# A graph-attention layer and a gated graph network: the ramp of a scheduled kernel, rearranged

## The chip, the cores and the metric

The kernel runs on one core of one Trainium2 chip. The metric is the device time of one execution in microseconds, as the median of several executions. An execution's time is a little longer than the span that its profile shows, from the first to the last instruction of the program.

## What is computed

The input is x, 32 sequences of 512 nodes with 128 features, in f32, and one adjacency matrix of 512 x 512 zeros and ones that all sequences share. Each of the two layers normalizes, clips at zero, runs a graph network and adds the result to its input:

```
h = max(layernorm(x), 0)
x = x + gat(h)          # layer 0
h = max(layernorm(x), 0)
x = x + ggnn(h)         # layer 1

gat(h):   hw = h @ W;  e_src = hw @ a_src;  e_dst = hw @ a_dst
          logits[i,j] = leaky_relu(e_src[i] + e_dst[j], 0.2)
          alpha = softmax over j, where adj[i,j] > 0
          return leaky_relu(alpha @ hw + b, 0.3)

ggnn(h):  five times:
          m = adj @ h                       # both halves of "av" are m
          z = sigmoid([m,m] @ w3.T + h @ u3.T + biases)
          r = sigmoid([m,m] @ w4.T + h @ u3.T + biases)
          v = tanh([m,m] @ w5.T + (r*h) @ u5.T + biases)
          h = (1-z)*h + z*v
```

## The kernel before

A sequence's 512 nodes are K = 4 groups of P = 128. The kernel doesn't write its instructions in the order of the loops. It makes a list of tasks first (`add`, line 320), each with an engine, the columns it works on, a key, the tasks it needs and the buffers it takes. A planner (`plan`, lines 79 to 129) then keeps a clock for each engine with the costs of `COST` (line 37), starts again and again the task that can begin first, and of those of one engine that can begin by then, the one with the lowest key. `at` holds a task back to a planned time. The tasks are issued in that order, and `pin` keeps the order of each engine as it was issued, so that each engine works through a queue fixed when the kernel is built, and waits where an operand isn't there yet. `BANKS` (line 48) counts the eight PSUM banks by use: m for aggregations, g for gates, v for candidates, o for all else.

**Before the first sequence.** SyncE (SP) issues the loads in the order x of sequence 0, the adjacency, x of 1 and 2, the weights, the biases (lines 413 to 418). ScalarE issues W (`gw`) and then the two score vectors a_src and a_dst (`avecs`, lines 394 to 396). TensorE has "idle" transposes (line 429): `FIRST_IDLE` of them may begin at a planned 700 ns, `IDLE` more at 8000, and their key of 1e12 lets any other work go first. The score vectors are spread over all partitions by a matmul with ones (`as_ps`, line 442), VectorE multiplies them with W and sums (`products`, line 452: wa = W a), and ScalarE writes wa beside W, which GpSimd (POOL) copied (lines 435 and 460 to 463). So `wrow` makes hw and the scores in one matmul. The adjacency is turned on TensorE in four blocks (`at_ps`, line 479), each copied from PSUM as f16 by ScalarE (`adjT`, line 487).

**Layer 0 of a sequence** (`layer0`, line 707) goes through these steps, each a task or a few:

- `relu_layernorm` (line 587): VectorE takes mean and variance of each group (599 to 606, ve is the variance plus epsilon), POOL raises ve to the power -0.5 (rs, line 614). With `first` (sequence 0), VectorE subtracts the mean (619) and then scales and clips all 512 columns (623). Otherwise VectorE makes nb = -mean * rs (630), and ScalarE scales, shifts and clips in four activations (638). It is used on x (names ending in a) and on x1, the result of layer 0 (names ending in b).
- `transposed` (line 648) turns h by four transposes on TensorE (655) and one ScalarE copy (658), for the first `DIRECT` = 4 sequences; later ones go through memory in blocks, by DMAs that POOL issues (`blockwise`, line 661).
- `product` (line 740): for each half of the groups, two matmuls make hp (749), and one ScalarE task takes the exponentials of the scores (755) and scales the two groups of hw by them (760).
- The exponentials of a node's scores are spread over the partitions (es): by transposes on TensorE for the first four sequences (`spread`, 774), through memory by POOL's DMAs (line and es) for the others.
- `weigh` (817): VectorE makes the weights pt of one group from es, hw and adjT; four of them. `average` (836): TensorE multiplies (av, 843), VectorE divides and adds the bias (rsum 870, o 872), then leaks (893) and adds x (896): x1.
- The second layer norm of x1, and its halves: hi is hN in f16 (ScalarE, 919), lo the remainder in f16 (VectorE, 917).

**Layer 1**, five steps of `recurrence` (line 923) for each sequence: TensorE aggregates hi and lo with adjT (m, 942), ScalarE copies (mT, 953), gates r and z (961, 962 and 982) and candidate (1000, 1001) follow with their tanh, and VectorE updates hT (974, 1012, 1018, 1021). hT is turned back on TensorE for the first and last sequences (1035), else through memory (1048 to 1059). Steps of several sequences are under way at once.

The instructions for an f32 matmul of the program appear twice in the profile, and those of its transposes once.

Of the kernel before, what the change touches and what calls it, by code (L numbers as in the profile page):

```python
# [15 lines left out]
P = 128  # L16
# [27 lines left out]
FIRST_IDLE, IDLE = 26, 30  # L44
# [234 lines left out]
def gat_then_gated_gnn_kernel(  # L279
# [40 lines left out]
    def add(*args, **kwargs):  # L320
        tasks.append(Task(*args, **kwargs))
        return tasks[-1]
# [71 lines left out]
    nc.scalar.dma_start(out=gw, in_=g_w)  # L394
# [19 lines left out]
    a_loaded = add("SP", [1], -9.8e9, lambda: load_rest("a"), lands=5800)  # L414
    xs[1] = load_x(1, -9.7e9, 6000)
    xs[2] = load_x(2, -9.6e9, 6200)
# [6 lines left out]
    f_idle = Buffer("o", "bank")  # L423
# [4 lines left out]
    for i in range(FIRST_IDLE + IDLE):  # L428
        add("PE", [480 if i < FIRST_IDLE else 256], 1e12, idle, (), (f_idle,),
            at=700 if i < FIRST_IDLE else 8000)  # L430
# [3 lines left out]
    def issue():  # L434
        pin(nc.gpsimd.tensor_copy(wrow[:, :D], gw))
        pin(nc.gpsimd.tensor_copy(wsrc[:, :D], gw))

    w_copied = add("POOL", [1], soon, issue, at=3600)
# [8 lines left out]
    t = add("PE", [1024], soon, issue, (), (f_as,), at=4100)  # L447
# [9 lines left out]
    wa_made = add("DVE", [150] * 2, -5.6 * STEP, issue, (t,), (f_as, f_products))  # L457
# [14 lines left out]
    def prepare_adjacency(c):  # L472

        f = Buffer("o", "bank")

        def turn():
            at_ps = new(f, f"at_ps{c}")
            for k in range(K):
                pin(nc.tensor.transpose(
                    at_ps[:, ts(k, P)],  # L480
                    a_sb[:, k, :].rearrange("p (q c) -> p c q", c=K)[:, c, :],
                    ident,
                ))

        t = add("PE", [512] * K, -4 * STEP + c, turn, (a_loaded,), (f,))
        adjacency.append(add(
            "ACT", [512], -4 * STEP + c, lambda: pin(nc.scalar.copy(adjT[:, c, :], f.tile)), (t,),
            (f,),
        ))
# [97 lines left out]
    def relu_layernorm(dst, src, which, keys, needs, buffers, first):  # L587
# [3 lines left out]
        def stats():  # L591
# [4 lines left out]
            st["nb"] = pools[3].tile([P, K], F32, tag="nb", name=f"nb_{which}")  # L596
# [6 lines left out]
        def aggr():  # L603
            for k in range(K):
# [4 lines left out]
            ))  # L609

        t = add("DVE", [128] * K, keys(0), stats, needs, buffers)
        t1 = add("DVE", [30] * K + [1], keys(1), aggr, (t,))
        t = add("POOL", [1, 1], keys(2),
                lambda: pin(nc.gpsimd.tensor_tensor(own["rs"], own["ve"], mhalf, ALU.pow)), (t1,))  # L614
        if first:
# [5 lines left out]
            def scale():  # L621
                by = own["rs"].rearrange("p (k o) -> p k o", o=1).to_broadcast([P, K, D])
                pin(nc.vector.scalar_tensor_tensor(dst(), dst(), 0.0, by, ALU.max, ALU.mult))

            t1 = add("DVE", [512], keys(2), centre, (t1,), buffers)
            return add("DVE", [512], keys(3), scale, (t, t1), buffers)


        def negated():
            pin(nc.vector.scalar_tensor_tensor(  # L630
                own["nb"], own["mv"][:, :, 0], -1.0, own["rs"], ALU.mult, ALU.mult
            ))

        t = add("DVE", [1], keys(3), negated, (t,))
# [8 lines left out]
        t = add("ACT", [280] * 2, keys(4), lambda: relu((0, 1)), (t,), buffers)  # L643
        return add("ACT", [280] * 2, keys(4), lambda: relu((2, 3)), (t,), buffers)
# [3 lines left out]
    def transposed(dst, src, which, keys, needs, buffers):  # L648

        f = Buffer("o", "bank")  # L650

        def turn():
            t_ps = new(f, f"t_{which}")
            for k in range(K):
                pin(nc.tensor.transpose(t_ps[:, ts(k, P)], src()[:, k, :], ident))

        t = add("PE", [256] * K, keys(0), turn, needs, (*buffers, f))
        return add("ACT", [512], keys(1), lambda: pin(nc.scalar.copy(dst(), f.tile)), (t,),
                   (*buffers, f))

    def blockwise(dst, src, which, keys, needs, buffers):
# [45 lines left out]
    def layer0(b):  # L707
# [21 lines left out]
        t = turn(hT, h, f"a{b}", keys, (t,), (f_h, f_hT))  # L729
# [10 lines left out]
        def product(half):  # L740
# [13 lines left out]
            def scale():  # L754
                pin(nc.scalar.activation(
                    hw()[:, 2 * half : 2 * half + 2, D:], hp2()[:, :, D:], AF.Exp
                ))
                for c in range(2):
# [3 lines left out]
            u = add("PE", [4 * (D + 3)] * 2, keys(half), multiply, (t, wrow_made), (f, f_hT))  # L762
            return add("ACT", [1, 160, 160], keys(1 + half), scale, (u,), (f, f_hw))

        made = [product(half) for half in range(K // 2)]
        base[0] = 12

        if direct:
            f_es = Buffer("o", "bank")

            def spread():
                es = new(f_es, f"es_{b}")
                for k in range(K):
                    pin(nc.tensor.transpose(
                        es[:, ts(k, P)], hw()[:, k, D + 1 : D + 2].to_broadcast([P, P]), ident
                    ))

            t = add("PE", [256] * K, keys(0), spread, made, (f_hw, f_es))
# [57 lines left out]
        def average(part):  # L836
# [40 lines left out]
            if direct:  # L877
                u = None
                for c in range(K):
                    u = add("PE", [4 * (D + 1)] * 2, keys(part), multiply_with(c),  # L880
                            (weighed[c], u), (f, f_hw, f_pts[c]))
            else:
                u = add("PE", [4 * (D + 1)] * 2 * K, keys(part), multiply, weighed,
# [22 lines left out]
        t = relu_layernorm(hN, lambda: x1, f"b{b}", keys, (t,), (f_hN,), b == 0)  # L906
        base[0] = 26
        halved = halves(b, hN, keys(0), (t,), (f_hN,))
        t = turn(lambda: hTs[b % SLOTS], hN, f"b{b}", keys, (t,), (f_hN,))
        return halved, t  # L910
# [326 lines left out]
```

## Time and profile before

| | |
|---|---|
| median of 3 runs | 1149.26 us (1147.39 to 1150.59) |
| the profiled execution | 1149.29 us, its span 1147.5 us |
| TensorE (PE) busy | 1137.7 us |
| VectorE (DVE) busy | 941.6 us |
| ScalarE (ACT) busy | 664.2 us |
| GpSimd (POOL) busy | 349.5 us |
| idle transposes on TensorE | 56, from 1.4 to 24.0 us of the span |

The page of a profile gives the busy time of each engine, the same in 40 slices, the DMA queues, the chain of work that ended last (followed back from the last instruction, at each step to what released it), and groups of like instructions with the idle time before them and what ended it. PE is TensorE's matmul side, PEld its loading of weights, which overlaps. Beside the page, the trace answers with timelines of any stretch, with the chain in order of time, and with busy times by stretches. A matmul's end is modelled, and matmuls overlap, so that the distance between two starts says more of TensorE's pace than a duration.

### The profile page before, as it was taken

The page shows a single profiled execution, that of the slowest core. Times are in us where ns is not written, and L with a number is a line of the kernel's source. Part 1 is how long each engine was busy: PE and PEld are TensorE (multiplying, and loading weights), DVE is VectorE, ACT ScalarE, POOL GpSimd, SP SyncE. Part 2 cuts the span into 40 slices and gives each one's busy share as a digit, 9 for nine tenths or more (in the row PEclk, how much of TensorE's full clock was granted, in tenths as well). Part 3 has the DMA queues.
Part 4 walks back from the last instruction along what each step waited for, and adds up shares of the span by engine and source line. Part 5 has one row for each costly group of instructions (what it writes and reads, how often), then busy time and mean ns, then how long its engine had stood idle before and what let it go on. Part 6 is the DMA issues. An engine that isn't in the chain of part 4 may idle for free.

```text
span 1147.5 us, 15090 instructions
## 1 busy us (share of the span) xinstructions
PE 1137.7 (99%) x4363; PEld 602.0 (52%) x4363; DVE 941.6 (82%) x2114; ACT 664.2 (58%) x1294; POOL 349.5 (30%) x501
## 2 busy tenths in 40 slices
PE   8999999999999999999999999999999999999998
PEld 8666555455455554545555454545555555444444
DVE  6879897878787987988988797889997988767664
ACT  5665556645655556565565756565556644555553
POOL 3354432242324325153243432135335331100000
PEclk9999999999999999999999999999999999999999
DMA  3123454444444544344444444444454443332311
GB/s 106 37 56 82 135 149 111 112 137 128 116 128 131 143 121 140 108 126 142 144 135 119 143 127 120 129 129 141 121 142 127 117 126 93 115 94 90 102 51 57
DMA packets 133915, 132.88 MB, mean 116 GB/s; under 512 B 22082, under 2 KB 97988, under 8 KB 133700
## 3 DMA queue, kind: packets, MB, share of 16 engines
q1 hardware_dynamic: 116208, 95.02, 26.4%
q0 software_dynamic: 17472, 36.79, 13.0%
q8 instruction: 36, 0.59, 0.2%
q14 instruction: 51, 0.42, 0.1%
q10 hardware_dynamic: 148, 0.07, 0.0%
HBM read 70.39 MB, written 61.40 MB: 115 GB/s over the span
## 4 chain that ended last, share of the span: by engine, by line
PE 93%; DVE 4%; ACT 1%; DMA 1%; issue 1%; SPq 0%; POOL 0%; ACTq 0%; DVEq 0%
PE m L942 23%; PE g L982 12%; PE g L961 11%; PE g L962 11%; PE v L1001 11%; PE v L1000 11%; PE av L843 9%; PE hp L749 2%; PE h L1035 0%; DVE hT L1021 0%; DVE pt L819 0%; DMA rows<-way 0%; DVE blocks L1048 0%; DMA avecs<-in_L_gnn_a_dst_dram 0%; DVE o L872 0%
## 5 line engine op out<-in xcount | busy, mean ns | idle before, releaser
L967 ACT ACTIVATE rs<-g,zrb 128x512 f32<-128x512 f32 x160 | 109.8, 687 | 144.8 <-PE g L962 139.1
L1006 ACT ACTIVATE hv<-v,vb 128x512 f32<-128x512 f32 x159 | 108.9, 685 | 110.7 <-PE v L1001 110.3
L982 PE MATMUL g<-mT,w3dT 128*128 128x512 f32 x320 | 164.0, 594 | 0.4 <-ACT rs L967 0.4
L961 PE MATMUL g<-hT,u3T 128*128 128x512 f32 x320 | 163.4, 592 | 0.0
L962 PE MATMUL g<-mT,w4sT 128*128 128x512 f32 x320 | 163.4, 592 | 0.0
L1000 PE MATMUL v<-mT,w5sT 128*128 128x512 f32 x318 | 162.4, 592 | 0.0
L1001 PE MATMUL v<-rh,u5hT 128*128 128x512 f32 x318 | 162.4, 592 | 0.0
L1012 DVE SCALAR_TENSOR_TENSOR d<-hv,hT 128x512 f32<-128x512 f32 x159 | 108.3, 681 | 64.6 <-ACT hv L1006 63.9
L942 PE MATMUL m<-adjT,lo 128*128 128x512 f16 x640 | 158.4, 379 | 0.4 <-DVE lo L917 0.3
L942 PE MATMUL m<-adjT,hi 128*128 128x512 f16 x640 | 157.7, 379 | 0.1
L989 ACT ACTIVATE zs<-g,zrb 128x512 f32<-128x512 f32 x160 | 109.7, 686 | 72.6 <-PE g L982 71.6
L953 ACT COPY mT<-m 128x512 f32<-128x512 f32 x160 | 93.6, 585 | 93.3 <-PE m L942 92.1
L974 DVE SCALAR_TENSOR_TENSOR rh<-rs,hT 128x512 f32<-128x512 f32 x160 | 108.4, 679 | 47.2 <-ACT rs L967 46.3
L843 PEld LDWEIGHTS av<-hw,pt 128*128 128x128 f32 x1024 | 123.2, 191 | 16.3 <-issue 10.0
L843 PE MATMUL av<-hw,pt 128*128 128x129 f32 x1024 | 124.4, 275 | 0.5 <-DVE pt L819 0.5
L1021 DVE SCALAR_TENSOR_TENSOR hT<-d,hT 128x512 f32<-128x512 f32 x159 | 109.7, 690 | 12.8 <-PE v L1001 0.5
L614 POOL TENSOR_TENSOR rs_b<-ve_b,mhalf 128x4 f32<-128x4 f32 x32 | 37.2, 1161 | 266.4 <-DVE ve_b L606 148.7
L1018 DVE SCALAR_TENSOR_TENSOR d<-zs,d 128x512 f32<-128x512 f32 x159 | 109.7, 690 | 4.8
L942 PEld LDWEIGHTS <-lo 128*128 128x128 f16 x640 | 62.4, 98 | 95.5 <-issue 38.2
L942 PEld LDWEIGHTS <-hi 128*128 128x128 f16 x640 | 62.6, 98 | 93.8 <-issue 37.1
L1048 DVE STREAM_TRANSPOSE blocks<-hT 128x512 f32<-128x512 f32 x146 | 102.9, 707 | 6.8 <-DMA way<-blocks 4.5
L962 PEld LDWEIGHTS g<-mT,w4sT 128*128 128x128 f32 x320 | 60.8, 190 | 76.5 <-issue 69.4
(133 smaller groups left out, 1447.1 us busy)
## 6 DMA issues: line engine op xcount, KB each, us to landing
way<-blocks SPq DMA_DIRECT2D x146, 256.0 KB, 2.1
rows<-way SPq DMA_DIRECT2D x584, 64.0 KB, 2.1
x<-in_x_dram SPq DMA_DIRECT2D x32, 256.0 KB, 2.9
out_dram<-res SPq DMA_DIRECT2D x31, 256.0 KB, 2.3
turn_a<-blocks_a POOLq DMA_DIRECT2D x112, 64.0 KB, 2.2
h0T<-turn_a POOLq DMA_DIRECT2D x28, 256.0 KB, 3.5
es<-line POOLq DMA_DIRECT2D x28, 256.0 KB, 4.0
turn_b<-blocks_b POOLq DMA_DIRECT2D x112, 64.0 KB, 2.2
```

The source lines that it names most:

```text
L843: pin(nc.tensor.matmul(avs()[:, i, :], lhsT=f_pts[c].tile[:, ts(2 * part + i, P)], rhs=hw()[:, c, : D + 1], start=start, stop=(c == K - 1) ...
L942: pin(nc.tensor.matmul(f_m.tile, lhsT=part[:, k, :], rhs=adjT[:, k, :], start=(first and k == 0), stop=(not first and k == K - 1),))
L961: pin(nc.tensor.matmul(g, lhsT=u3T, rhs=hT, start=True, stop=False))
L962: pin(nc.tensor.matmul(g, lhsT=w4sT, rhs=f_mT.tile, start=False, stop=True))
L967: pin(nc.scalar.activation(new(f_r, f"rs_{b}_{step}"), f_g.tile, AF.Tanh, bias=rb, scale=0.5))
L982: pin(nc.tensor.matmul(f_g.tile, lhsT=w3dT, rhs=f_mT.tile, start=False, stop=True, skip_group_check=True))
L989: pin(nc.scalar.activation(new(f_z, f"zs_{b}_{step}"), f_g.tile, AF.Tanh, bias=zb, scale=0.5))
L1000: pin(nc.tensor.matmul(v, lhsT=w5sT, rhs=f_mT.tile, start=True, stop=False))
L1001: pin(nc.tensor.matmul(v, lhsT=u5hT, rhs=f_rh.tile, start=False, stop=True))
L1006: pin(nc.scalar.activation(new(f_hv, f"hv_{b}_{step}"), f_v.tile, AF.Tanh, bias=vb))
L1018: pin(nc.vector.scalar_tensor_tensor(d, f_z.tile, 1.0, d, ALU.add, ALU.mult))
L1021: pin(nc.vector.scalar_tensor_tensor(hT, f_d.tile, 0.5, hT, ALU.mult, ALU.add))
```

## The change

Nothing of what is computed changes. The edits are these:

- The score vectors are ScalarE's first loads; W is loaded by SP, after x of sequence 0. ScalarE copies W into `wrow` and `wsrc` instead of POOL. Planned times of the loads and of the first tasks are set anew, and there are 32 and 36 idle transposes instead of 26 and 30, the second group from a planned 6500 ns; their bank is of kind v.
- Adjacency: the banks of kind g are used, blocks 1 and 3 are copied by VectorE, 0 and 2 by ScalarE, with new keys; blocks 2 and 3 are held back to a planned 9900.
- Layer norm: except for sequence 0's first, VectorE makes nm = -mean and POOL makes nb = nm * rs right after rs. Sequence 0's first scales in two halves. Sequence 0's second is no longer `first`: ScalarE's activations do it.
- Transposes of h are two tasks of two; for the first norm of sequence 0 the copy is in halves too.
- The exponentials of hw are a task of their own for each half, and the scalings follow as other tasks; for the first four sequences they need the exponentials of both halves. The averages need the scalings. es for those sequences takes a bank of kind g and is made in two tasks.

As the planner decides the order, the queues of all engines differ over their whole length; the last twenty instructions of TensorE stand in the same order. In the new queue of TensorE, the "idle" transposes stand at 19 places, the last after some 1840 rows of about 3970. The diff, cut to its core:

```diff
@@ -43,3 +43,3 @@
 }
-FIRST_IDLE, IDLE = 26, 30
+FIRST_IDLE, IDLE = 32, 36
 LANDING = 2600
@@ -393,3 +393,2 @@
-    nc.scalar.dma_start(out=gw, in_=g_w)
     for i, v in enumerate((g_asrc, g_adst)):
@@ -413,5 +412,6 @@
     xs = {0: load_x(0, -9.9e9, 3200)}
-    a_loaded = add("SP", [1], -9.8e9, lambda: load_rest("a"), lands=5800)
-    xs[1] = load_x(1, -9.7e9, 6000)
-    xs[2] = load_x(2, -9.6e9, 6200)
+    add("SP", [1], -9.85e9, lambda: pin(nc.sync.dma_start(out=gw, in_=g_w)))
+    a_loaded = add("SP", [1], -9.8e9, lambda: load_rest("a"), lands=5000)
+    xs[1] = load_x(1, -9.7e9, 5000)
+    xs[2] = load_x(2, -9.6e9, 5100)
     rest_loaded = add("SP", [1] * 6, -9.5e9, lambda: load_rest("rest"), (xs[2][1],), lands=3000)
@@ -422,3 +422,3 @@
-    f_idle = Buffer("o", "bank")
+    f_idle = Buffer("v", "bank")
@@ -429,3 +429,3 @@
         add("PE", [480 if i < FIRST_IDLE else 256], 1e12, idle, (), (f_idle,),
-            at=700 if i < FIRST_IDLE else 8000)
+            at=700 if i < FIRST_IDLE else 6500)
@@ -434,6 +434,6 @@
     def issue():
-        pin(nc.gpsimd.tensor_copy(wrow[:, :D], gw))
-        pin(nc.gpsimd.tensor_copy(wsrc[:, :D], gw))
+        pin(nc.scalar.copy(wrow[:, :D], gw))
+        pin(nc.scalar.copy(wsrc[:, :D], gw))
-    w_copied = add("POOL", [1], soon, issue, at=3600)
+    w_copied = add("ACT", [128, 128], soon, issue, at=4200)
     f_as, f_products = Buffer("o", "bank"), Buffer("d")
@@ -446,3 +446,3 @@
-    t = add("PE", [1024], soon, issue, (), (f_as,), at=4100)
+    t = add("PE", [1024], soon, issue, (), (f_as,), at=3900)
@@ -456,3 +456,3 @@
-    wa_made = add("DVE", [150] * 2, -5.6 * STEP, issue, (t,), (f_as, f_products))
+    wa_made = add("DVE", [150] * 2, -5.6 * STEP, issue, (t,), (f_as, f_products), at=4400)
@@ -473,3 +473,4 @@
-        f = Buffer("o", "bank")
+        f = Buffer("g", "bank")
+        key = (0.2 * c - 3.8) * STEP
@@ -484,7 +485,7 @@
-        t = add("PE", [512] * K, -4 * STEP + c, turn, (a_loaded,), (f,))
-        adjacency.append(add(
-            "ACT", [512], -4 * STEP + c, lambda: pin(nc.scalar.copy(adjT[:, c, :], f.tile)), (t,),
-            (f,),
-        ))
+        t = add("PE", [256] * K, key, turn, (a_loaded,), (f,), at=9900 if c > 1 else 0)
+        engine, copy = ("DVE", nc.vector.tensor_copy) if c % 2 else ("ACT", nc.scalar.copy)
+        adjacency.append(
+            add(engine, [512], key, lambda: pin(copy(adjT[:, c, :], f.tile)), (t,), (f,))
+        )
@@ -595,3 +596,5 @@
             st["rs"] = pools[3].tile([P, K], F32, tag="rs", name=f"rs_{which}")
-            st["nb"] = pools[3].tile([P, K], F32, tag="nb", name=f"nb_{which}")
+            if not first:
+                st["nm"] = pools[3].tile([P, K], F32, tag="nm", name=f"nm_{which}")
+                st["nb"] = pools[3].tile([P, K], F32, tag="nb", name=f"nb_{which}")
             own.update(st)
@@ -609,2 +612,4 @@
             ))
+            if not first:
+                pin(nc.vector.tensor_scalar(own["nm"], own["mv"][:, :, 0], -1.0, None, ALU.mult))
@@ -612,4 +617,8 @@
         t1 = add("DVE", [30] * K + [1], keys(1), aggr, (t,))
-        t = add("POOL", [1, 1], keys(2),
-                lambda: pin(nc.gpsimd.tensor_tensor(own["rs"], own["ve"], mhalf, ALU.pow)), (t1,))
+        def power():
+            pin(nc.gpsimd.tensor_tensor(own["rs"], own["ve"], mhalf, ALU.pow))
+            if not first:
+                pin(nc.gpsimd.tensor_tensor(own["nb"], own["nm"], own["rs"], ALU.mult))
+        t = add("POOL", [1, 1], keys(2), power, (t1,))
         if first:
@@ -620,16 +629,17 @@
-            def scale():
-                by = own["rs"].rearrange("p (k o) -> p k o", o=1).to_broadcast([P, K, D])
-                pin(nc.vector.scalar_tensor_tensor(dst(), dst(), 0.0, by, ALU.max, ALU.mult))
+            def scale(half):
+                def issue():
+                    two = slice(2 * half, 2 * half + 2)
+                    by = own["rs"][:, two].rearrange("p (k o) -> p k o", o=1)
+                    pin(nc.vector.scalar_tensor_tensor(
+                        dst()[:, two, :], dst()[:, two, :], 0.0, by.to_broadcast([P, 2, D]),
+                        ALU.max, ALU.mult,
+                    ))
+                return issue
             t1 = add("DVE", [512], keys(2), centre, (t1,), buffers)
-            return add("DVE", [512], keys(3), scale, (t, t1), buffers)
+            return [add("DVE", [256], keys(3), scale(i), (t, t1), buffers) for i in range(2)]
-        def negated():
-            pin(nc.vector.scalar_tensor_tensor(
-                own["nb"], own["mv"][:, :, 0], -1.0, own["rs"], ALU.mult, ALU.mult
-            ))
-        t = add("DVE", [1], keys(3), negated, (t,))
@@ -642,4 +652,6 @@
-        t = add("ACT", [280] * 2, keys(4), lambda: relu((0, 1)), (t,), buffers)
-        return add("ACT", [280] * 2, keys(4), lambda: relu((2, 3)), (t,), buffers)
+        return [
+            add("ACT", [280] * 2, keys(4), lambda: relu((0, 1)), (t,), buffers),
+            add("ACT", [280] * 2, keys(4), lambda: relu((2, 3)), (t,), buffers),
+        ]
@@ -647,3 +659,3 @@
-    def transposed(dst, src, which, keys, needs, buffers):
+    def transposed(dst, src, which, keys, needs, buffers, by_halves):
@@ -651,12 +663,23 @@
-        def turn():
-            t_ps = new(f, f"t_{which}")
-            for k in range(K):
-                pin(nc.tensor.transpose(t_ps[:, ts(k, P)], src()[:, k, :], ident))
+        def turn(half):
+            def issue():
+                t_ps = f.tile or new(f, f"t_{which}")
+                for k in range(2 * half, 2 * half + 2):
+                    pin(nc.tensor.transpose(t_ps[:, ts(k, P)], src()[:, k, :], ident))
+            return issue
-        t = add("PE", [256] * K, keys(0), turn, needs, (*buffers, f))
-        return add("ACT", [512], keys(1), lambda: pin(nc.scalar.copy(dst(), f.tile)), (t,),
-                   (*buffers, f))
+        def copy(of):
+            return lambda: pin(nc.scalar.copy(dst()[:, of], f.tile[:, of]))
-    def blockwise(dst, src, which, keys, needs, buffers):
+        t = [add("PE", [256] * 2, keys(0), turn(i), (needs[i],), (*buffers, f)) for i in range(2)]
+        if not by_halves:
+            t = add("ACT", [512], keys(1), copy(slice(0, N)), t, (*buffers, f))
+            return [t, t]
+        return [
+            add("ACT", [256], keys(1), copy(ts(i, N // 2)), (t[i],), (*buffers, f))
+            for i in range(2)
+        ]
+    def blockwise(dst, src, which, keys, needs, buffers, by_halves):
@@ -728,3 +751,3 @@
         turn = transposed if direct else blockwise
-        t = turn(hT, h, f"a{b}", keys, (t,), (f_h, f_hT))
+        t = turn(hT, h, f"a{b}", keys, t, (f_h, f_hT), b == 0)
@@ -753,3 +776,3 @@
-            def scale():
+            def exponentials():
                 pin(nc.scalar.activation(
@@ -757,2 +780,4 @@
                 ))
+            def scale():
                 for c in range(2):
@@ -761,6 +786,13 @@
-            u = add("PE", [4 * (D + 3)] * 2, keys(half), multiply, (t, wrow_made), (f, f_hT))
-            return add("ACT", [1, 160, 160], keys(1 + half), scale, (u,), (f, f_hw))
-        made = [product(half) for half in range(K // 2)]
+            needs = (t[half], wrow_made) if direct else (t, wrow_made)
+            u = add("PE", [4 * (D + 3)] * 2, keys(half), multiply, needs, (f, f_hT))
+            u = add("ACT", [1], keys(0.9 + 0.1 * half), exponentials, (u,), (f, f_hw))
+            return u, scale, f
+        made, scales, f_hps = zip(*(product(half) for half in range(K // 2)))
+        scaled = [
+            add("ACT", [160, 160], keys(2 + i), scales[i], made if direct else (made[i],),
+                (f_hps[i], f_hw))
+            for i in range(2)
+        ]
         base[0] = 12
@@ -768,12 +800,17 @@
         if direct:
-            f_es = Buffer("o", "bank")
+            f_es = Buffer("g", "bank")
-            def spread():
-                es = new(f_es, f"es_{b}")
-                for k in range(K):
-                    pin(nc.tensor.transpose(
-                        es[:, ts(k, P)], hw()[:, k, D + 1 : D + 2].to_broadcast([P, P]), ident
-                    ))
+            def spread(half):
+                def issue():
+                    es = f_es.tile or new(f_es, f"es_{b}")
+                    for k in range(2 * half, 2 * half + 2):
+                        pin(nc.tensor.transpose(
+                            es[:, ts(k, P)], hw()[:, k, D + 1 : D + 2].to_broadcast([P, P]), ident
+                        ))
+                return issue
-            t = add("PE", [256] * K, keys(0), spread, made, (f_hw, f_es))
+            t = None
+            for half in range(2):
+                t = add("PE", [256] * 2, keys(0), spread(half), (made[half], t), (f_hw, f_es))
         else:
@@ -880,5 +917,5 @@
                     u = add("PE", [4 * (D + 1)] * 2, keys(part), multiply_with(c),
-                            (weighed[c], u), (f, f_hw, f_pts[c]))
+                            (weighed[c], scaled[c // 2], u), (f, f_hw, f_pts[c]))
             else:
-                u = add("PE", [4 * (D + 1)] * 2 * K, keys(part), multiply, weighed,
+                u = add("PE", [4 * (D + 1)] * 2 * K, keys(part), multiply, (*weighed, *scaled),
                         (f, f_hw, *f_pts))
@@ -905,7 +942,7 @@
-        t = relu_layernorm(hN, lambda: x1, f"b{b}", keys, (t,), (f_hN,), b == 0)
+        t = relu_layernorm(hN, lambda: x1, f"b{b}", keys, (t,), (f_hN,), False)
         base[0] = 26
-        halved = halves(b, hN, keys(0), (t,), (f_hN,))
-        t = turn(lambda: hTs[b % SLOTS], hN, f"b{b}", keys, (t,), (f_hN,))
-        return halved, t
+        halved = halves(b, hN, keys(0), t, (f_hN,))
+        t = turn(lambda: hTs[b % SLOTS], hN, f"b{b}", keys, t, (f_hN,), False)
+        return halved, t[0] if direct else t
```

## The prediction

> **What bounds the kernel now.** I read the busy rows of the page first, then the chain of waits, then the same chain cut to the first 30 us, and last the table of busy time by stretches.
>
> ```profile
> PE 1137.7 (99%) x4363; PEld 602.0 (52%) x4363; DVE 941.6 (82%) x2114; ACT 664.2 (58%) x1294; POOL 349.5 (30%) x501
> ...
> PE 93%; DVE 4%; ACT 1%; DMA 1%; issue 1%; SPq 0%; POOL 0%; ACTq 0%; DVEq 0%
> ```
>
> TensorE carries 93% of the chain. A busy row hides holes, because matmuls overlap and fillers count as work. So I counted TensorE's lost time from its starts in the timeline: unbroken runs start a 128x128 f32 instruction every 0.109 us, 128x129 and 128x131 every 0.112, 128x512 f16 every 0.216, 128x512 f32 every 0.429; whatever a start lies beyond that, and every "idle" transpose whole, is lost. The span then splits into 1.4 us before the first start, 16.2 lost up to 45 us, 2.8 lost from there to the last start at 1142.7 (0.4 of it at 1139.8, the rest in a dozen holes of 0.1 to 0.6), 4.8 after that start, and 1122.3 of work that the change leaves alone. 1.4 + 16.2 + 2.8 + 4.8 + 1122.3 = 1147.5. Outside the ramp there are 2.8 us to win or lose; the ramp has 16.2, of which 13.2 by 24.7 us. Its chain:
>
> ```profile
> 1.76 4.41 DMA avecs<-in_L_gnn_a_dst_dram
> ...
> 6.30 1.19 PE as_ps L442 x2
> 7.49 2.11 PE idle L426 x9
> 9.60 0.85 PE at_ps L479 x4
> 10.46 0.85 PE t_a L655 x4
> 11.31 1.70 PE at_ps L479 x8
> 13.01 0.89 PE hp L749 x8
> 13.90 0.11 PE idle L426
> 14.01 0.48 PE at_ps L479 x4
> 14.49 0.44 PE idle L426 x4
> 14.93 0.44 PE es L774 x4
> 15.36 0.98 PE idle L426 x9
> 16.35 3.35 PE av L843 x28
> 19.70 0.02 issue
> 19.72 0.18 DVE rsum L870
> ```
>
> The columns are start, length and what. The last score vector lands at 6.17; everything up to hp stands in TensorE's queue behind it, and those transposes take 0.213 us each. hp's four (x8) take 0.112: TensorE doubled its speed at 12.80.
>
> ```profile
> 20.00:25.00 5.00, 4.91 (x44) 4.62 (x43) 4.83 (x19) 3.48 (x13) 0.81 (x1) 1.00 0.16 54
> 25.00:30.00 5.00, 4.60 (x31) 3.38 (x31) 4.88 (x12) 2.73 (x9) 0.57 (x1) 1.00 0.00 0
> ...
> 40.00:45.00 5.00, 4.16 (x29) 3.33 (x30) 4.86 (x17) 2.40 (x8) 2.26 (x3) 1.00 0.04 17
> ```
>
> After the stretch, the columns are its length and busy PE, PEld, DVE, ACT, POOL. From 20 us VectorE is full (4.8 of 5), so TensorE's last ramp holes are waits for VectorE: an earlier start counts only if VectorE too is ahead.
>
> [...] In the trace a_src, issued at 1.25, landed at 3.95, and a_dst, issued at 1.76, only at 6.17, among the packets of the adjacency (landed 6.36).
>
> **Part by part** (the profiled execution: 1149.29 us, its span 1147.5 and 1.8 around it; the median 1149.26 is the same).
>
> *Loads.* Without gw ahead, a_dst takes a_src's place on ACT's queue (1.25) and lands near 3.95. gw goes to SP behind x of sequence 0; its issue moves the adjacency and x of 1 and 2 by 0.42 (the issue of one load), to 6.8, 7.3 and 8.0. Sixteen fillers end at 1.36 + 16 x 0.213 = 4.8, so as_ps starts at 4.8 instead of 6.3, and the hole is gone. W's two copies on ScalarE (0.37 each, as its 128x128 scalings) lie between W's landing near 4.2 and wa at 6.6, when ScalarE has nothing else; without that cover they would delay the four wa copies by 0.7, still ahead of h0T. The other kinds of bank cost nothing: g's gates begin after 25 us.
>
> *Clock.* [...] I take 5.97. Then: as_ps to 5.97, nine fillers to 6.95, two adjacency blocks (8 x 0.12) to 7.9, t_a (4 x 0.109) to 8.35.
>
> *First sequence in halves.* VectorE and POOL are not last: products after as_ps at 6.1, rs_a at 6.58 as now, two halves of 0.36 done at 7.3. ScalarE's halves of h0T follow their two transposes (0.2 after the start of the second): about 0.37 each from its 0.59 for 512, done at 8.7 and 9.0. hp starts at 8.75 instead of 12.80: -4.05. At 9.39: hp at 10.4, -2.4.
>
> *Exponentials apart.* Now from hp to pt 2.7 us (12.81 to 15.49): the second exponential waits for two scalings (0.63). Without them es would be done 1.75 after hp's start, but VectorE must first finish norms a1 and a2 and an adjacency copy: 7.3 + 2 x (0.87 + 0.40 + 0.17) + 0.65 = 10.9, so 2.1: -0.55. The scalings (x4, about 1.2) end before the first averages' weights do.
>
> *Adjacency by two engines.* No row shows VectorE copying PSUM to f16. Between 0.59 (ScalarE's copy) and 0.75 (pt): 0.65. One of its two copies stands between pt 0 and pt 1: +0.65 there, with the three pts behind it. Now, averages end 1.5 after the last pt, as 32 x 0.112 is longer than four pts; then they follow it by 0.75. Together 0. rsum then starts at 15.3 instead of 19.72: -4.4.
>
> *Layer-norm bias by POOL.* A product 128x4: 0.18 by the row of zrb's product, between 0.1 and 0.3 (its 128x128 copy is 0.29); 63 of them, 11 us on an engine busy 349.5. Queued behind each are POOL's DMA issues (turn, line, es): 0.2 later, beside loads of 2 to 4 us. VectorE's nm costs what nb did (0.15), its waits for POOL (3.2 us, all told) go. For the second norm of sequence 0, VectorE loses centre and scale (2 x 0.69), ScalarE gains four activations (4 x 0.40): about 1 us later on that path, to which VectorE's 1.4 is the return. VectorE's sum: +1.3 copies, -1.4, 0.
>
> *Order and fillers.* There are 12 more fillers. They stand where TensorE's order has nothing ready; up to twelve times 0.109 = 1.3 would be lost if one stood ahead of ready work. Walking the new order on with the same durations: ve of norm b comes 4.4 after rsum as now, 19.7; pow and product (1.4 and 0.2, with 0.2 between) end at 21.5, four activations at 23.2, hi (0.6) at 23.8; TensorE has fillers and averages of sequence 1 meanwhile; m's high part runs 23.9 to 24.7, four averages follow, the low part ends near 26.0 instead of 29.7, with 16.1 us of real work issued by then where 29.7 has 14.2: 5.5 ahead. Part of it goes again where VectorE is full (about 19 us of its work from norm b of sequence 0 to the second low part, as now, and x of 3 and 4 with it) and to the late fillers; I keep 4.1. The last twenty instructions are in the same order, so the 4.8 stay. 1149.3 - 4.1 = 1145.2.
>
> **Rivals.** *Late clock:* [...] -2.4 at 9.39, -1.6 at 12.8: 1147 to 1148. [...] *Given back:* VectorE at 4.8 of 5 does the same work up to 45 us, so TensorE waits for it there as long as it gained; 1149. Against: VectorE itself starts its full stretch 4 us earlier. *Slower:* the scalings, now tasks behind the exponentials, come late for the averages of the 28 sequences whose rows go through memory. One such wait costs what the hole of 0.48 at 964.8 cost; in all 28, 13.4 - 4.1 makes 1158.5; it decides from 16 of them on (7.7, the gain and 3.4 more). Against: es takes 4.0 from issue to landing after the exponentials, scalings 0.63, ScalarE is 58% busy.
>
> **Numbers.** About 0.3%, 3.4 us, is what a measurement here tells from no change: faster means below 1145.8. Forecast 0.53 (1143.5 to 1146.5, a tenth of it above 1145.8); late clock 0.28; given back 0.10; slower 0.07; more than forecast (all 5.5 kept, fewer later holes; 1142.5) 0.02. Faster 0.48 + 0.02 = 0.50; slower 0.07; same 0.43. The range reaches over the first three cases, with the later holes 0.5 either way: 1142.5 to 1149.5.
>
> **What would show it.** as_ps near 4.8; the step from 0.213 to 0.109 at about 6; hp at 8.8, rsum at 15.3; 12 us lost up to 45 us instead of 16.2. Wrong if avecs still land after 5, if the step comes at 9 or later, if ScalarE's scalings release av, or if the holes after 45 us sum to more than 4.

## The result and the profile after

The changed kernel takes 1156.11 us (median of 5 runs, 1155.04 to 1158.41) where the kernel before takes 1149.26 (5 runs, 1147.39 to 1150.59): a ratio of 1.0069, with a 95% interval of 1.0058 to 1.0080. The prediction was 1145.2, with a range up to 1149.5.

The page of the changed kernel shows hardly anything: the same busy times, VectorE even 0.5 us less, POOL 27 us more.

```profile
PE 1139.0 (99%) x4375; PEld 601.3 (52%) x4375; DVE 941.1 (82%) x2116; ACT 661.9 (57%) x1299; POOL 376.4 (33%) x562
...
PE 86%; DVE 6%; DMA 3%; POOL 2%; ACT 1%; issue 1%; DVEq 0%; SPq 0%; POOLq 0%; ACTq 0%
```

The second line, the chain's shares, is the one that speaks: TensorE had 93% of the chain and has 86% now. VectorE, DMA and POOL took the rest, so TensorE must have waited for them. Counting TensorE's lost time from its starts, as the prediction did:

| us | before | after |
|---|---|---|
| ahead of the first start | 1.4 | 1.4 |
| lost up to 45 us | 16.2 | 11.8 |
| lost from 45 us to the last start | 2.8 | 12.8 |
| after the last start | 4.8 | 5.8 |
| work | 1122.3 | 1122.3 |
| span | 1147.5 | 1154.1 |

The ramp lost 4.4 us less, and the stretch behind it 10 more. First the ramp, in the chain of the changed kernel cut to its first 40 us (start, length, what):

```profile
1.37 3.68 PE idle L426 x16
5.04 1.15 PE as_ps L442 x2
6.19 2.11 PE idle L426 x9
8.31 1.42 PE at_ps L480 x8
9.73 0.45 PE t_a L668 x4
10.18 0.02 issue
10.20 0.38 ACT h0T L673
10.58 0.04 issue
10.62 1.16 PE hp L772 x8
```

The wait for the score vectors is gone, as_ps follows the fillers at once, and hp starts at 10.62 instead of 12.80. The busy times of the three stretches that the prediction showed of before (length, then PE, PEld, DVE, ACT, POOL) are now:

```profile
20.00:25.00 5.00, 5.00 (x47) 4.96 (x45) 4.93 (x18) 3.54 (x12) 1.22 (x2) 1.00 0.17 52
25.00:30.00 5.00, 5.00 (x35) 3.86 (x35) 4.68 (x26) 3.42 (x9) 2.80 (x4) 1.00 0.01 2
40.00:45.00 5.00, 5.00 (x26) 3.02 (x24) 2.67 (x14) 2.08 (x6) 2.53 (x4) 1.00 0.07 13
```

TensorE is full in all three, and from 40 to 45 VectorE no longer is. Now the later stretch. From 60 to 1130 us, TensorE of the kernel before has two holes of over 0.25 us; the changed kernel has eight (1.0 us at 477.8, 3.1 at 536.2, 0.7 at 565, 0.7 at 586, 0.6 at 672, 1.4 at 844, 1.1 at 876, 0.6 at 896). The longest shows how it comes about. First ScalarE's timeline, then the chain, both of the changed kernel (nb_b is the bias of the second layer norm, rs_b its power):

```profile
533.65 0.63 ACT L785 ACTIVATE hw<-hp,hw 128x128 f32<-128x128 f32 x2
536.61 0.88 ACT L648 ACTIVATE hN<-x,nb_b,rs_b 128x128 f32<-128x128 f32 x2 [2.33 <-POOL nb_b L621]
537.39 0.67 ACT L1043 ACTIVATE hv<-v,vb 128x512 f32<-128x512 f32 x1
537.96 0.16 ACT L778 ACTIVATE hw<-hp 128x6 f32<-128x6 f32 x1
538.15 0.63 ACT L785 ACTIVATE hw<-hp,hw 128x128 f32<-128x128 f32 x2
538.67 0.62 ACT L956 CAST hi<-rows 128x512 f16<-128x512 f32 x1
```

```profile
534.55 1.41 POOL rs_b L619
535.96 0.07 issue
536.03 0.56 POOL nb_b L621
536.58 0.03 issue
536.61 0.88 ACT hN L648 x2
537.48 0.57 ACT hv L1043
...
538.67 0.63 ACT hi L956
539.29 0.05 issue
539.34 1.69 PE m L979 x7
```

ScalarE's queue had reached the activation of a layer norm whose power POOL had not begun. It stood for 2.33 us, and behind it in the queue stood the copy hi of another sequence, for which TensorE waited: the line of TensorE's waits is

```profile
PE m L979 <- ACT hi L956: 3.3, 2, 2.9
PE g L1019 <- ACT rs L1004: 1.8, 3, 0.9
PE g L998 <- DMA hT<-turn_b: 1.5, 2, 0.9
```

(total, times, longest). The holes at 478, 586 and 896 have the same kind of chain: power, product, two or four activations of the norm, a gate's tanh (rs, L1004), TensorE. Those at 565 and 876 end with hT, which a DMA brings from memory, the one at 672 with a copy hi, the one at 844 with VectorE. ScalarE's waits for the bias, first in the kernel before and then in the changed one, are

```profile
ACT hN L638 <- DVE nb_b L630: 7.7, 9, 1.8
ACT h L638 <- DVE nb_a L630: 5.4, 6, 2.1
...
ACT h L648 <- POOL nb_a L621: 11.7, 8, 4.0
ACT hN L648 <- POOL nb_b L621: 10.7, 12, 2.3
```

They sum to 13.1 us before and 22.4 after.

### The profile page after: what moved, and what is told of

Read it like the earlier page. It is cut to its first block, busy times and chain, and to the rows that moved or that the text cites. A ratio compares the mean times of both kernels' runs of the same rounds, so it can differ in the third digit from the quotient of the medians.

```text
span 1154.1 us, 15378 instructions
## 1 busy us (share of the span) xinstructions
PE 1139.0 (99%) x4375; PEld 601.3 (52%) x4375; DVE 941.1 (82%) x2116; ACT 661.9 (57%) x1299; POOL 376.4 (33%) x562
## 4 chain that ended last, share of the span: by engine, by line
PE 86%; DVE 6%; DMA 3%; POOL 2%; ACT 1%; issue 1%; DVEq 0%; SPq 0%; POOLq 0%; ACTq 0%
PE m L979 21%; PE g L1019 11%; PE g L998 10%; PE v L1038 10%; PE g L999 10%; PE v L1037 10%; PE av L880 9%; PE hp L772 2%; PE idle L426 1%; DMA rows<-way 1%; DVE pt L856 1%; DVE blocks L1085 1%; POOL rs_b L619 1%; DVE hT L1058 1%; DVE d L1055 1%
## 5 line engine op out<-in xcount | busy, mean ns | idle before, releaser
L1004 ACT ACTIVATE rs<-g,zrb 128x512 f32<-128x512 f32 x160 | 109.7, 685 | 148.3 <-PE g L999 148.0
L979 PE MATMUL m<-adjT,hi 128*128 128x512 f16 x640 | 160.4, 379 | 3.3 <-ACT hi L956 3.3
L1058 DVE SCALAR_TENSOR_TENSOR hT<-d,hT 128x512 f32<-128x512 f32 x159 | 109.9, 691 | 12.5 <-PE h L1072 0.5
L1038 PEld LDWEIGHTS v<-rh,u5hT 128*128 128x128 f32 x318 | 60.2, 190 | 78.1 <-issue 60.5
```

The source lines that it names most:

```text
L979: pin(nc.tensor.matmul(f_m.tile, lhsT=part[:, k, :], rhs=adjT[:, k, :], start=(first and k == 0), stop=(not first and k == K - 1),))
L1004: pin(nc.scalar.activation(new(f_r, f"rs_{b}_{step}"), f_g.tile, AF.Tanh, bias=rb, scale=0.5))
L1038: pin(nc.tensor.matmul(v, lhsT=u5hT, rhs=f_rh.tile, start=False, stop=True))
L1058: pin(nc.vector.scalar_tensor_tensor(hT, f_d.tile, 0.5, hT, ALU.mult, ALU.add))
```

## The experiments

Theory A: the bias edit does it. The activation needs POOL's power and product, which end later than the planner reckons, and ScalarE and then TensorE stand behind it. The rival, theory B: the order does it. Any edit makes the planner draw another order of some 4000 instructions, and some orders have more holes than others, whatever was edited. The median of before lies between 1147.4 and 1149.3 in the different sessions, so each run is given by its ratio to before in its own session.

**The order held, the engine changed.** Two runs take the engine apart from the order. The first makes nb on VectorE, with every queue of TensorE, ScalarE and SP kept exactly as in the changed kernel:

```diff
-            if not first:
-                pin(nc.gpsimd.tensor_tensor(own["nb"], own["nm"], own["rs"], ALU.mult))
...
         def relu(ks):
+            if 0 in ks:
+                pin(nc.vector.scalar_tensor_tensor(
+                    own["nb"], own["mv"][:, :, 0], -1.0, own["rs"], ALU.mult, ALU.mult
+                ))
             for k in ks:
```

> The changed kernel with every queue's order kept, but nb made by VectorE (one instruction right ahead of the ScalarE activations that need it) instead of POOL's product, and nm dropped. Theory A, late bias (POOL's power and product end later than the planner reckons, and ScalarE's queue stands behind the activation that waits for them, TensorE behind ScalarE): the holes in TensorE after 45 us fall from 12.3 us to some 5, 1149 us. Theory B, order (a new order meets new holes, whatever was edited): the holes stay, 1155 to 1157.

1156.22 us, ratio 1.0073 (1.0059 to 1.0087). Not one us is won in the median. Five of the eight holes stand at the same places (0.9 at 480, 2.0 at 538, 0.6 at 671, 1.2 at 842, 0.4 at 895); those at 565, 586 and 876 are gone, and one of 0.7 at 721 is new. From 45 to 1130 us this profile loses 9.3 us where the changed kernel's lost 12.3, and up to 45 us it loses 13.8 instead of 11.8. At 538, nb comes sooner, and ScalarE stands for less, but it stands:

```profile
535.74 0.62 ACT L785 ACTIVATE hw<-hp,hw 128x128 f32<-128x128 f32 x2
537.48 0.88 ACT L648 ACTIVATE hN<-x,nb_b,rs_b 128x128 f32<-128x128 f32 x2 [1.12 <-DVE nb_b L644]
```

So theory A as I had it has fallen: the holes were to shrink to some 5 us without POOL's product, and most of them stay. ScalarE's waits for nb are even longer here, 32.0 us in all. The activation is too early in ScalarE's queue, whoever makes nb.

**The bias edit undone, planned anew.** nb is a VectorE task of the plan again, all else is as in the change:

```diff
-            if not first:
-                pin(nc.gpsimd.tensor_tensor(own["nb"], own["nm"], own["rs"], ALU.mult))
...
+        t = add("DVE", [1], keys(3), negated, (t,))
```

> The changed kernel with the bias edit alone undone (nb as a VectorE task, planned anew). Theory A: 1145 to 1147, all of the ramp's gain stays. Theory B: anywhere from 1145 to 1156, since the order is new again.

1145.53 us, ratio 0.9981 (0.9974 to 0.9987). By the ratios this is 0.88%, some 10 us, less than the changed kernel, and 2.2 us less than before. TensorE loses 0.6 us between 45 and 1130; apart from the start, the only wait of over 0.1 that its list of waits has is at the end:

```profile
PE idle L426 <- POOL ident masks.py:199: 1.4, 1, 1.4
PE h L1075 <- DVE hT L1061: 0.2, 1, 0.2
```

**The converse.** That plan kept, with the VectorE task left in it but empty, and nm and nb made as in the change, on VectorE and POOL:

```diff
+        t = add("DVE", [1], keys(3), lambda: None, (t,))
```

> The converse of the order-held run: planned as if VectorE made nb (that task stays in the plan, empty), so the queues of TensorE, ScalarE and SP are those of the 1145.5 us version, but nm comes from VectorE and nb from POOL right after the power. Theory A1 (the plan's missing step is the cause: without it ScalarE's activations are queued too early, whoever makes nb): 1145 to 1147. Theory A2 (POOL's product itself is late): 1150 or more.

1147.00 us, ratio 0.9991 (0.9982 to 0.9999). With this order, POOL's product costs about 0.1%, some 1 us, and the two intervals overlap. By the ratios the order is worth 9 to 11 us, the engine 0 to 1. What the edit took from the plan is a step: in the plan, power to activation was 1300 + 130 ns of POOL, then 71 + 140 of VectorE and its queueing there; now it is 1300 + 130 alone. Call this A1: without this planned time ("the step" from here on) the planner puts ScalarE's activations into the queue too early, whoever makes nb.

**The bias edit alone, on the kernel before.**

> The kernel before with the bias edit alone (nm by VectorE, nb by POOL right after the power). Theory A: slower by 5 to 9, 1154 to 1158, with waits of ScalarE for nb up from 13 us to over 20. Theory B: as likely 1148 as 1156.

1151.65 us, ratio 1.0034 (1.0021 to 1.0048): slower, though by less than expected. ScalarE's waits for nb are 29.7 us against 13.1, TensorE's loss between 45 and 1130 is 7.6 against 2.3.

**A re-plan with no change of work.** Only the numbers of fillers change in the kernel before:

```diff
-FIRST_IDLE, IDLE = 26, 30
+FIRST_IDLE, IDLE = 32, 36
```

> The kernel before with 32 and 36 idle transposes instead of 26 and 30 and nothing else: a re-plan with next to no change of work. Theory A: within 1 us of 1149. Theory B: off by several us in either direction, if the planner's order changes after the ramp.

1147.68 us, ratio 1.0000 (0.9991 to 1.0009). But this draw's order is near the old one: 76 of TensorE's 4307 instructions, fillers left out, stand elsewhere, against some 2100 in the changed kernel. So it says little on B.

**Planned time given back.** In the changed kernel, nb on POOL, the plan holds what follows the power back by 211 ns more, and by 1000 more:

```diff
-        t = add("POOL", [1, 1], keys(2), power, (t1,))
+        t = add("POOL", [1, 1], keys(2), power, (t1,), lands=130 if first else 341)
```

> The changed kernel, nb on POOL, with 211 ns more planned between the power task and what needs it, which is what the VectorE task had added (71 of cost, 140 of landing). Theory A1: most of the loss goes, 1146 to 1150. Theory B, the order's luck: anywhere from 1146 to 1157.

1148.10 us, ratio 1.0000 (0.9991 to 1.0008): as A1 expects, though B's range holds it too. TensorE's loss from 45 to 1130 is about 5 us against 12.3; ScalarE's waits for nb, which A1 would have fall, are 19.7 against 22.4.

> The same with 1000 ns more. Theory A1: 1145 to 1147, ScalarE's waits for nb under 10 us where the changed kernel has 22. Theory B: anywhere from 1146 to 1157.

1157.12 us, ratio 1.0082 (1.0068 to 1.0097): a miss. ScalarE's waits for nb do fall, to 4.6 us, but TensorE waits elsewhere. The longest wait of its list is

```profile
PE g L998 <- DMA hT<-turn_b: 3.1, 1, 3.1
```

at 144 us. In the chain there, POOL issues the load of a sequence's hT behind another norm's power (1.49 us), and the load takes 4.88: hT comes too late for the first step. The planned time may be wrong on either side, or the draw was bad; one run doesn't tell.

**Other draws.** The changed kernel and the 1145.5 us version, both with the old 26 and 30 fillers:

> The changed kernel with 26 and 30 idle transposes as before: a re-plan that has nothing to do with the bias. Theory A1: still 1154 to 1157, since the early activations stay. Theory B: another draw, 1146 to 1157.

1152.00 us, ratio 1.0029 (1.0015 to 1.0042): faster than A1 had it, and inside B's range.

> The 1145.5 us version with 26 and 30 idle transposes: a re-plan with the VectorE task for nb in the plan. Theory A1: 1144.5 to 1148, clearly under the 1152.0 of the same two edits with nb on POOL. Theory B: as likely over 1150 as under.

1151.06 us, ratio 1.0025 (1.0015 to 1.0036). Here A1 missed: the step is in the plan, and the holes are there too (6.1 us between 45 and 1130, the longest 1.4 at 114). Luck of the order is real, and the 10 us between the first two forms can't all be the bias edit. So three more twins were run, each with one number of the plan moved in both forms, which gives both a new order: a DMA's landing 2700 for 2600, ScalarE's landing 170 for 160, VectorE's 150 for 140. Their edits are these single lines:

```diff
-LANDING = 2600
+LANDING = 2700
...
-    "DVE": (70, 1.055, 140),
-    "ACT": (150, 0.83, 160),
+    "DVE": (70, 1.055, 150),
+    "ACT": (150, 0.83, 170),
```

> The changed kernel with the planner's time for a DMA's landing at 2700 ns instead of 2600, which moves its order and nothing of the work. Theory A1 (no planned step between power and activations: queued too early): 1150 to 1157, and slower than its twin with the VectorE task. Theory B (the order's luck alone): no matter which twin.

1155.62 us, ratio 1.0057 (1.0044 to 1.0071).

> The twin of pool_landing with nb as a VectorE task in the plan. Theory A1: faster than pool_landing by 2 or more. Theory B: either sign.

1148.97 us, ratio 1.0003 (0.9994 to 1.0011).

> The changed kernel with ScalarE's landing at 170 ns in the plan instead of 160. Theory A1: 1150 to 1157 and slower than its twin. Theory B: either.

1149.94 us, ratio 1.0009 (1.0000 to 1.0017), a hair under A1's range.

> The twin of pool_act with nb as a VectorE task in the plan. Theory A1: faster than pool_act by 2 or more. Theory B: either sign.

1146.66 us, ratio 0.9975 (0.9964 to 0.9985).

> The changed kernel with VectorE's landing at 150 ns in the plan instead of 140. Theory A1: 1150 to 1157 and slower than its twin. Theory B: either.

1150.69 us, ratio 1.0023 (1.0013 to 1.0032).

> The twin of pool_dve with nb as a VectorE task in the plan. Theory A1: faster than pool_dve by 2 or more. Theory B: either sign.

1147.36 us, ratio 0.9996 (0.9988 to 1.0005). All twins together, with what the traces show of each (ScalarE's waits for nb, TensorE's loss from 45 to 1130, both in us). The ratios are of medians; waits and losses are those of one profiled execution each, which for the 26 and 30 without the step was 2.7 us faster than its median:

| plan | no step (nb on POOL): ratio, waits, loss | step (nb on VectorE): ratio, waits, loss |
|---|---|---|
| the change, 32 and 36 fillers | 1.0069, 22.4, 12.3 | 0.9981, 12.5, 0.6 |
| the same, 26 and 30 | 1.0029, 24.1, 4.9 | 1.0025, 15.4, 6.1 |
| landing 2700 | 1.0057, 30.8, 11.4 | 1.0003, 13.7, 3.5 |
| ScalarE 170 | 1.0009, 32.9, 9.0 | 0.9975, 10.6, 1.9 |
| VectorE 150 | 1.0023, 19.7, 6.9 | 0.9996, 16.3, 2.7 |
| the kernel before | 1.0034, 29.7, 7.6 | 1, 13.1, 2.3 |

The form without the step is slower in six pairs of six, by 0.04 to 0.88%, 0.40% on average or 4.6 us. The pair at 0.04% is not told apart, and from the spread of the six pairs the average is known to some 0.3% only (an estimate of a 95% interval: 0.1 to 0.7%, 1 to 8 us). The waits of ScalarE are longer without the step in all six, but within a column they don't rank the times: the longest, 32.9, stand beside the smallest ratio, 1.0009. Within one form the draw alone moves the time by 0.6% (1.0009 to 1.0069) or 0.5% (0.9975 to 1.0025). In the five pairs of the change, the ratios average 1.0037 without the step and 0.9996 with it. So both theories hold a part: of the 6.9 us, the missing step is worth about 4.6 on average, with the 0 to 1 of the engine in it, which the twins change as well, and the rest is the draw.

**Parts of the ramp.** The load order and W's copies alone, on the kernel before:

```diff
-    nc.scalar.dma_start(out=gw, in_=g_w)
...
+    add("SP", [1], -9.85e9, lambda: pin(nc.sync.dma_start(out=gw, in_=g_w)))
...
-        pin(nc.gpsimd.tensor_copy(wrow[:, :D], gw))
+        pin(nc.scalar.copy(wrow[:, :D], gw))
```

> The kernel before with the loads' order alone (score vectors first, W by SP, W copied by ScalarE, planned times of these as in the change). The part as I priced it: as_ps near 4.9, TensorE's full clock by 9.4, first hp at 11.5 or sooner, and 1.5 to 3 us less lost up to 45 us than in a run of before whose clock comes at 12.8: 1145 to 1147. If the clock's step is not tied to the hole before as_ps: within 1 us of before.

1151.54 us, ratio 1.0034 (1.0020 to 1.0048), slower: both expectations missed. as_ps starts at 4.89 and hp at 9.59, as priced. But up to 45 us TensorE loses 12.6, and behind it 4.5 instead of 2.3. The profile is that of the fastest of seven executions (1148.98; the slowest took 1154.60), so what the slower ones lose isn't shown.

The new order of the loads has a price of its own. With W ahead of it on SP, the adjacency lands at 7.1 to 8.9 us in all sixteen profiles of plans with this order, where it lands at 6.3 to 6.6 in the four with the old one. In twelve of the sixteen TensorE is there first and waits for it. The longest is in the first of the order-held runs, where two starts of TensorE are 2.8 us apart:

```profile
PE at_ps L480 <- DMA a_sb<-in_adj_dram: 2.5, 1, 2.5
```

In the changed kernel's own profile the adjacency landed at 7.65 and TensorE's fillers, nine from 6.12 on at 0.22 us each, stood until 8.1, so the wait doesn't show.

Exponentials and scalings as one task again, in the 1145.5 us version:

```diff
-            u = add("ACT", [1], keys(0.9 + 0.1 * half), exponentials, (u,), (f, f_hw))
+            return add("ACT", [1, 160, 160], keys(1 + half), scale, (u,), (f, f_hw))
```

> The 1145.5 us version (bias edit undone) with exponentials and scalings in one task again. As I priced the split: es and pt of the first sequence some 0.5 us later, 1146; if the new order matters more, 1144 to 1149.

1146.61 us, ratio 0.9985 (0.9977 to 0.9992): no difference from 0.9981 shows in this one plan. Lost up to 45: 13.0 against 12.7.

**The kernel before, in another execution.**

> The kernel before, looked at again: at what time TensorE's starts go from 0.213 to 0.109 us apart. [...] another time than 12.8, later than 9.7 [...].

One time, 1147.05 us, and a profile with another ramp. The chain up to hp, in the same columns as before:

```profile
6.28 0.67 PE as_ps L442 x2
6.95 1.14 PE idle L426 x9
8.09 0.48 PE at_ps L479 x4
8.57 0.44 PE t_a L655 x4
9.00 0.96 PE at_ps L479 x8
9.97 0.98 PE hp L749 x8
```

as_ps is where it was, but the nine fillers take 1.14 us instead of 2.11, and t_a's four transposes 0.44 instead of 0.85: the pace that the first profile has from 12.8 us on is there by 7.0. The pace is there with as_ps already, whose two instructions start 0.29 us apart, against 0.56 in the first profile. The trace also keeps a record of the granted clock, which begins with its first rise: 5.5 us here, inside the hole ahead of as_ps (from 5.0 to 6.3), and 12.9 in the first profile. This run loses 13.2 us up to 45 where the first profile lost 16.2, with not one instruction changed. And my bound, later than 9.7, missed; no trace had shown a ground for it. The two other plans with the old ramp have the rise at 6.0 (32 and 36 fillers) and at 5.8 (the bias edit alone), and lose 12.4 and 12.0 up to 45.

## Why the prediction was wrong

It was wrong in sign. The step that failed is the price of the new order: it was put at 0.5 us either way behind the ramp, and the bias edit, which takes a task out of the plan and so changes that order, was put at nothing. The runs with the order held show 9 to 11 us for the order and 0 to 1 for the engine. Two of the prediction's own signs of being wrong came true: the pace doubled at 9.3 only, and the holes behind 45 us sum to more than 4. Point by point:

- *The bound* was right as a sum: TensorE's lost time and its work, 1122.3 us in both, account for both spans. That there were only 2.8 us to win or lose outside the ramp was wrong (see the order, below).
- *Loads*: half right. as_ps stands at 4.97 (4.8 priced) and the hole is gone. But the adjacency, priced to land at 6.8, landed at 7.65, and up to 8.9 in other executions. In twelve of the sixteen profiles with this order it is the next wait, 2.5 us in the longest.
- *Clock*: the reasoning failed. The granted clock rose at 9.3 in the changed kernel's profile, where I took 5.97; this is what the late-clock rival said, which put the time at 1147 to 1148 for it. I had taken the 12.80 of one profile as if it were the kernel's; what put the rise at 5.97, or at 9.39 in a second case, no trace had shown. Over the profiles the rise comes at 12.9, 5.5, 6.0 and 5.8 with the old order of loads and anywhere from 4.2 to 10.9 in the sixteen with the new one, so its time differs from execution to execution, and what sets it isn't shown. The hole before as_ps did not hold it back: in three of the four profiles with the old order (5.5, 6.0 and 5.8) the rise came inside the hole, in the fourth 6.6 us after its end at 6.30.
- *Halves*: right. h0T comes in halves of 0.38 (0.37 priced), and hp starts at 10.62, where the late-clock rival had 10.4.
- *Exponentials apart*: right in the ramp. From hp to the first pt it takes 2.0 us (2.1 priced, 2.7 before). Over the whole kernel no gain of it shows (0.9985 without the split, 0.9981 with it).
- *Adjacency by two engines*: the copy took 0.69 (0.65 taken), and the term was mis-sized: pt 0 to rsum takes 4.8 us, not 4.2. I had let the averages follow the last pt by 0.75; it is 1.3, as TensorE turns two adjacency blocks first and begins the averages at 13.5. rsum stands at 17.44. I had written 15.3, a gain of 4.4; the terms themselves, 4.05 and 0.55, make 4.6.
- *Lost up to 45 us*: 11.8, where 16.2 - 4.1 makes 12.1. The number was right by luck: the 16.2 has a late clock in it. The three other profiles with the old ramp lose 13.2, 12.4 and 12.0, an average of 12.5; the fifteen with the changed ramp (one of them without the split) lose 10.1 to 13.8, an average of 12.5 too. The ramp's edits show a gain of 0 to 1 us, not of 4. rsum says the same: it stands at 16.8 in those three, and at 16.2 to 18.5 in the fifteen. The longer way from pt 0 to rsum and the wait for the adjacency took back what the earlier starts gave.
- *Layer-norm bias by POOL*: "A product 128x4: 0.18 ... 63 of them, 11 us on an engine busy 349.5" was costed at nothing beside other work. The product's medians are 0.20 and 0.28 us, but single ones take up to 0.72, and all 63 take 20.7 us; with the order held this costs 0 to 1 us in all. What I left out is that the edit removes a task from the plan. What the plan is left with between ve and the activation, 1430 ns and 140 for VectorE's landing, is little more than the median of what it takes (0.06 + 1.04 + 0.07 + 0.20 + 0.03 = 1.40 us) and less than the 2.13 at the longest hole. The removed task's 211 ns and its queueing had been a margin. How much of the wait of 2.33 us there they would have covered isn't shown; ScalarE stood there before the power had begun.
- *Order and fillers*: "with the later holes 0.5 either way" is the term of the sum that carried the error: 12.3 us are lost from 45 to 1130, where I kept 2.3. I had read the 2.8 us of loss behind the ramp as all that can be lost there. It is what one drawn order loses, and others lose 0.6 to 13.
- *The slower rival* had the right side and the wrong mechanism. No scaling ends a wait in the changed kernel's list for TensorE's matmuls; its holes end with other work of ScalarE (behind the layer norm's activations in four of eight), with a DMA and with VectorE.

With the bias left on VectorE, the same edits give 1145.53 us. That this is near the forecast of 1145.2 is chance: the kernel before took 1147.48 in that session, so the gain is 2.2 us and not 4.1, and the four other draws of that form (1.0025, 1.0003, 0.9975, 0.9996) average 1.0000 of before. That version, and its twin with ScalarE's landing at 170 (0.9975, 0.9964 to 0.9985), beat both kernels.

What stays open: that the order costs the time, and not the engine, is shown by the orders held. That the missing step makes orders worse is shown on average only, by six pairs with a wide interval. How it does so, by early activations of ScalarE, is seen in the chains of four of eight holes, but the sum of the waits doesn't rank the times. That just the 211 ns of the plan are missing is supported by one run (1148.1) and was not tried over several draws. What of the order makes the holes at 565, 672, 844 and 876 wasn't settled.

## What to carry to other kernels

Where an order is written by a planner and then held by in-order queues, an edit can act twice, as here: on the engine (0 to 1 us), and on the order (9 to 11 us). Taking a task out of a plan also takes out its planned time, which may have been the margin that kept a waiting instruction from the head of a shared queue; hold the order and swap the engine to see which of the two acts. Compare such edits over several plans drawn with a number moved that should not matter: here the draw alone is worth 0.5 to 0.6%, more than the 0.36% that the edits were meant to win.

## What the hardware showed beside

The granted clock of TensorE rose anywhere from 4.2 to 12.9 us after the program's start, execution by execution. The two profiles of the kernel before, with the rise at 12.9 and at 5.5, lost 16.2 and 13.2 us up to 45 us. In three of the twenty profiles the clock fell again, from about 8 us on, after TensorE had stood 1.3 us for the adjacency; in the run that stood 2.7 us it did not. One of the three is VectorE's landing at 150 without the step, where the mean of 9 to 12 us is 0.54 (the third number from the end is the mean granted clock of the stretch):

```profile
9.00:12.00 3.00, 3.00 (x16) 2.78 (x15) 2.19 (x13) 1.16 (x3) 0.19 (x1) 0.54 0.30 76
```

In one run a hole late in the kernel cost twice. After the hole of 3.3 us at 144.5 in the run with 1000 ns more, TensorE's timeline shows two pairs of 128x512 f32 matmuls that take 1.76 and 1.91 us, beside 1.10 and 1.17 for the pairs around them, and the mean granted clock of that stretch is 0.50:

```profile
147.82 1.10 PE L998 MATMUL g<-hT,u3T 128*128 128x512 f32 x2 [3.13 <-DMA hT<-turn_b]
148.76 1.76 PE L999 MATMUL g<-mT,w4sT 128*128 128x512 f32 x2
150.31 1.91 PE L998 MATMUL g<-hT,u3T 128*128 128x512 f32 x2
152.02 1.17 PE L999 MATMUL g<-mT,w4sT 128*128 128x512 f32 x2
...
149.00:152.00 3.00, 3.00 (x4) 1.01 (x3) 0.72 (x2) 1.19 (x2) 0.58 (x2) 0.50 0.27 61
```

The starts from 149.5 to 152.0 are 0.853 us apart instead of 0.429: about 1.7 us more were lost. The hole of 3.1 us at 536.2 in the changed kernel has no such stretch behind it: the mean granted clock from 539 to 548 is 1.00. POOL's power of 128x4 took from 1.01 to 1.55 us in the changed kernel and its product from 0.19 to 0.72, on inputs of one size.
